# Softmax weights turned in 32 by 32 blocks and carried by DMA, with the gate's products on TensorE, in a cross-attention and expert kernel

## The chip, the cores and the metric

The kernel runs on one core of one Trainium2 chip. The metric is the device time of one execution in microseconds: the median of three runs for the kernel before, and one further execution that a hardware profiler recorded. PE is TensorE, DVE is VectorE, ACT is ScalarE, POOL is GpSimd and SP is SyncE, which here only issues DMAs.

## The reference

One layer of gated cross-attention, followed by a mixture of experts. All data is float32.

```python
# x (32, 112, 256), ctx (32, 375, 256); 16 heads of 64; 8 experts of width 1024, the best 2 of them
lat = layer_norm(layernorm(x)) * g_l + b_l          # 112 latents per batch: the queries
med = layer_norm(ctx) * g_m + b_m                   # 375 rows
q = lat @ Wq
k, v = split(concat([med, lat]) @ Wkv)              # 487 keys per batch
attn = softmax(q @ k.T * 64 ** -0.5)                # per batch and head: 112 x 487
x = x + tanh(g_xattn) * (concat_heads(attn @ v) @ Wout)
xn = layernorm(x)
scores = softmax(xn @ gate_w)                       # 8 experts per token
top2, idx = top_k(scores, 2); top2 /= sum(top2)
y = sum over the two: top2 * (gelu(xn @ w1[e] + b1[e]) @ w2[e] + b2[e])
x = x + tanh(g_ffn) * y
```

## The kernel before

The work has two parts. The first is attention over 32 batches, in a loop over 128 steps n (line 1370). One step handles the softmax of one batch for two pairs of heads, so four heads; `heads_of` (445) says which. Eight steps make a group g of two batches, and m is the step's place in it. The second part, from line 1551 on, is the expert layer over blocks of gathered tokens.

K and V of two batches are computed together by `seven` (361): seven products on PE in place of eight, whose sums DVE and POOL form. Its parts p1, p6, p7, p5 and then three `last` parts are spread over the five slots of a step, K's in one step and V's in the next. The last part p5 ends with two additions on POOL (`add`, 402).

Softmax runs one step ahead. In step n `scores(n + 1)` (451) puts 112 x 487 scores of a pair of heads into PSUM and DVE finds their maxima; `exps` (472) takes the exponentials on ACT into `ex`, with queries on partitions; `norm` (487) multiplies by the reciprocal sums on ACT, for the first pair in slot 1 and for the second in slot 3. Within step n, `turn_attn(n, h)` (494) then turns the weights of the step's own heads: per head four PE transposes of 112 x 122, written to PSUM, and one copy to `exT`, on DVE for three heads and on ACT for one. In every even step `attend` (505) multiplies V with the turned weights of the two steps before, which gives the heads' outputs, in 64 matmul records.

When a tile of 128 tokens is complete, `project` (539), `residual` (556) and `normed` (574) finish attention for it, and `logits_of` (581) forms the gate's eight products per token as eight multiply-and-sum instructions on DVE. `route_parts` (603) finds the two experts, and POOL scatters the rows to DRAM.

The order of instructions is written out by hand (`manual_schedule`, 1262). Each engine runs its instructions in the order in which the program names them, and so does SP's queue of DMAs. In a step that order is: loads for a later batch and zero fills of the gathered rows (`fill`, 168; three at n = 4, three at n = 8, two at n = 12, 3.64 MB each), then for n from 44 to 108 the weight pieces (`piece_out`, `piece_in`, 1204 to 1257: four stores to DRAM and two loads per step; POOL forms their sums in slots 2 and 3), then `attend`, `scores` and `exps` of the next step, and the slots. At n = 126 `others` (1183) takes over the space of the attention weights and loads the first expert's weights and three blocks of rows, all from SP.

Of the kernel before, what the change touches and what calls it, by code (L numbers as in the profile page):

```python
# [18 lines left out]
DH = 64  # L19
# [4 lines left out]
def kernel(  # L24
# [56 lines left out]

    NCK = 4
    KC = (NK + NCK - 1) // NCK
    NKP = NCK * KC
    keys = [(c * KC, min(KC, NK - c * KC)) for c in range(NCK)]

# [16 lines left out]
    gwd = dram.tile([E, D], F32, name="gwd")  # L103
# [60 lines left out]
    gw_sb = const.tile([P, E, D], F32, name="gw_sb")  # L164
# [10 lines left out]
    if True:  # L175
# [9 lines left out]
        ps_s = at.enter_context(tc.tile_pool(name="ps_s", bufs=2, space=PSUM))  # L185
# [105 lines left out]

        def turn(b, k, eng=None):

            if b % 2 == 0 and k == 0:
                kvT[b // 2] = kvp.tile([P, KD, 2, NKP], F32, tag="kvT", name=f"kvT_{b}")
                nc.gpsimd.memset(kvT[b // 2][:, :, :, NK:], 0.0)
            ps = ps_m.tile([P, 512], F32, tag="m", name=f"ps_turn_{b}_{k}")
# [16 lines left out]
        def q_unit(g, i):  # L314

            qT[g, i] = qk.tile([P, 2, S], F32, tag="qT", name=f"qT_{g}_{i}", bufs=6)
# [9 lines left out]
            nc.scalar.mul(qT[g, i], ps, DH**-0.5)  # L326
# [9 lines left out]
        def input_sums(g):  # L336

            (a0, b0), (a1, b1) = ([kvT[g][:, k, u, :] for u in range(2)] for k in range(KD))
            tT[g] = kvp.tile([P, 4, NKP], F32, tag="tT", name=f"tT_{g}")
            t1, t2, t3, t4 = (tT[g][:, n, :] for n in range(4))  # L340
# [20 lines left out]
        def seven(kv, j):  # L361
# [5 lines left out]
            (a0, _), (a1, b1) = ([kvT[g][:, k, u, :] for u in range(2)] for k in range(KD))  # L367
            t1, t2, t3, t4 = (tT[g][:, n, :] for n in range(4))
            v = {}

            def new(at, n):
                if kv == 0:
                    if n is None:
                        v[at] = qk.tile([P, NK], F32, tag="tmpk", name=f"tmpk_{j}", bufs=1)
# [4 lines left out]
                elif n is None:  # L379
                    v[at] = qk.tile([KC, NCK, P], F32, tag="tmpv", name=f"tmpv_{j}", bufs=1)  # L380
                else:
                    v[at] = vv[j][:, :, n[0] - a, n[1] // NG, :]

            def product(n, w, x):
# [5 lines left out]
                else:  # L390
                    ps = ps_m.tile([KC, NCK, P], F32, tag="m", name=f"ps_v_{j}_{n}")
                    for c in range(NCK):
                        nc.tensor.matmul(  # L393
                            ps[:, c, :],
                            lhsT=x[:, c * KC : (c + 1) * KC],
# [9 lines left out]
            def p1():  # L405
                if kv == 1:
                    vv[j] = proj.tile([KC, NCK, 2, 2, P], F32, tag="vv", name=f"vv_{j}")
# [30 lines left out]
        pss, nmx, ex, sm, exT = {}, {}, {}, {}, {}  # L438

        exs = [[const.tile([S, 2, NKP], F32, name=f"ex_{n}_{p}") for p in range(2)] for n in range(2)]  # L440
        for n in range(2):
            for p in range(2):
# [1204 lines left out]
```

## Time and profile before

| | |
|---|---|
| median of three runs | 2115.97 us (2115.82 to 2121.14) |
| profiled execution | 2118.11 us |
| its span, granted clock | 2116.3 us, 0.998 |
| DMA moved | 193.89 MB, mean 92 GB/s |

The span is the time from the first to the last instruction in the trace; the execution's own time includes a little around it. In lines of the profile, "L499" is a line of the kernel, "x2048" the number of instructions, and the names are those of the tiles. The heaviest groups that the change touches, from the page:

| line | engine | what | count | busy us | mean ns |
|---|---|---|---|---|---|
| L499 | PE | transposes of the weights | 2048 | 281.0 | 259 |
| L503 | DVE | copy of the turned weights | 384 | 237.0 | 617 |
| L503 | ACT | the same, one head in four | 128 | 66.3 | 518 |
| L586 | DVE | the gate's products | 224 | 116.4 | 520 |
| L478 | ACT | exponentials, 487 columns | 512 | 337.5 | 667 |
| L492 | ACT | normalisation, 487 columns | 512 | 331.1 | 694 |
| L468 | DVE | maxima, 974 elements | 256 | 287.9 | 1166 |

Busy time of PE is modelled: it takes in the pipeline's latency, so that matmuls overlap in it. The distance between the starts of two instructions is what one of them costs a full queue.

### The profile page before, as it was taken

To read this page: it belongs to the slowest core of one execution; us is meant where nothing else is said; L and a number is where in the kernel's file an instruction comes from. 1 tells how busy PE (TensorE), PEld (TensorE's weight loads), DVE (VectorE), ACT (ScalarE), POOL (GpSimd) and SP (SyncE) were. 2 spreads that over 40 slices of the span, in tenths; PEclk is the share of its full clock that TensorE was granted. 3 is DMA by queue.
4 is the path that set the end of the run, shared out by engine and by line. 5 is a ranking of instruction groups with operands and counts; after the bars stand their busy time and mean duration, and the time that the engine had idled before them with its cause. 6 is when DMAs were issued, how large, how long until landed. Compare 5 with 4: busy or idle time off the path is not lost. (4 is left out here: it accounts for less than half of the span.)

```text
span 2116.3 us, 44362 instructions
## 1 busy us (share of the span) xinstructions
PE 2084.2 (98%) x16232; PEld 1644.0 (78%) x16232; DVE 1367.9 (65%) x2985; ACT 1194.0 (56%) x2817; POOL 965.8 (46%) x1412
## 2 busy tenths in 40 slices
PE   9999999999999999999999999999999999999998
PEld 5777777777777777777777777777777799999887
DVE  6667676767676767676767676767666578655211
ACT  5666565656665666566666666565655433444433
POOL 5532323333345544554535553653233367877312
PEclk9999999999999999999999999999999999999999
DMA  6693000000002211221112211120002257699773
GB/s 151 186 321 109 15 16 18 13 22 27 18 25 65 86 41 53 63 82 53 55 55 58 73 55 55 57 76 4 8 4 68 98 152 221 170 322 299 195 213 59
DMA packets 201027, 193.89 MB, mean 92 GB/s; under 512 B 25856, under 2 KB 170824, under 8 KB 200680
## 3 DMA queue, kind: packets, MB, share of 16 engines
q1 hardware_dynamic: 188344, 174.65, 27.1%
q0 software_dynamic: 11328, 15.33, 3.7%
q8 instruction: 130, 2.13, 0.4%
q10 hardware_dynamic: 1136, 1.05, 0.2%
q14 instruction: 89, 0.73, 0.1%
HBM read 168.20 MB, written 65.76 MB: 111 GB/s over the span
## 5 line engine op out<-in xcount | busy, mean ns | idle before, releaser
L492 ACT ACTIVATE ex<-ex,rc 112x487 f32<-112x487 f32 x512 | 331.1, 694 | 328.2 <-DVE rc L490 325.3
L468 DVE TENSOR_REDUCE nmx<-ps_s 112x2 f32<-112x974 f32 x256 | 287.9, 1166 | 311.9 <-PE ps_s L458 310.9
L478 ACT ACTIVATE ex<-ps_s,nmx 112x487 f32<-112x487 f32 x512 | 337.5, 667 | 159.7 <-DVE nmx L468 157.3
L499 PEld LDWEIGHTS ps_t<-ident,ex 112*122 112x122 f32 x2048 | 232.4, 138 | 120.1 <-issue 96.4
L499 PE MATMUL ps_t<-ident,ex 112*122 112x112 f32 x2048 | 281.0, 259 | 1.0 <-ACT h L1001 1.0
L403 POOL TENSOR_TENSOR vv<-tmpv,vv 122x512 f32<-122x512 f32 x64 | 81.4, 1271 | 415.1 <-ACT vv L421 331.5
L503 DVE COPY exT<-ps_t 122x448 f32<-122x448 f32 x384 | 237.0, 617 | 37.9 <-PE ps_t L499 36.7
L458 PE MATMUL ps_s<-kT,qT 64*112 64x487 f32 x1024 | 242.0, 591 | 0.0
L513 PEld LDWEIGHTS ps_o<-exT,vv 122*64 122x64 f32 (+1 forms) x4096 | 197.6, 136 | 44.8 <-DVE kT L417 33.0
L513 PE MATMUL ps_o<-exT,vv 122*64 122x112 f32 (+1 forms) x4096 | 211.4, 260 | 0.0
L393 PE MATMUL ps_v<-wkv_s,tT 128*122 128x128 f32 x1536 | 202.3, 275 | 1.2 <-DVE vv L417 1.2
L403 POOL TENSOR_TENSOR kT<-tmpk,kT 128x487 f32<-128x487 f32 x63 | 76.8, 1219 | 269.7 <-ACT kT L421 269.7
L387 PE MATMUL ps_k<-tT,wkv_s 128*128 128x487 f32 x378 | 189.4, 583 | 4.1 <-ACT qT L326 3.5
L393 PEld LDWEIGHTS ps_v<-wkv_s,tT 128*122 128x122 f32 x1536 | 181.9, 185 | 4.2 <-issue 1.8
L393 PEld LDWEIGHTS ps_v<-wkv,kvT 128*122 128x122 f32 x1024 | 125.8, 185 | 74.3 <-issue 56.7
L1018 POOL DMA_INDIRECT out_dram<-y,xs x60 | 93.5, 1559 | 156.9 <-DVE y L1042 93.6
L427 DVE TENSOR_TENSOR kT<-ps_k,kT 128x487 f32<-128x487 f32 x189 | 124.6, 659 | 48.2 <-PE ps_k L387 41.9
L427 DVE TENSOR_TENSOR vv<-ps_v,vv 122x512 f32<-122x512 f32 x192 | 131.5, 685 | 35.5 <-PE ps_v L393 28.4
L458 PEld LDWEIGHTS ps_s<-kT,qT 64*112 64x112 f32 x1024 | 81.1, 172 | 79.5 <-issue 63.2
L393 PE MATMUL ps_v<-wkv,kvT 128*122 128x128 f32 x1024 | 139.0, 279 | 1.0 <-DVE kT L427 1.0
L387 PE MATMUL ps_k<-kvT,wkv 128*128 128x487 f32 x252 | 130.2, 598 | 0.0
L1243 POOL TENSOR_TENSOR piece<-piece 128x128 f32<-128x128 f32 x256 | 120.0, 469 | 16.5 <-DMA piece<-in_L_ffn_w_dram 2.5
(288 smaller groups left out, 3943.8 us busy)
## 6 DMA issues: line engine op xcount, KB each, us to landing
w<-in_L_ffn_w_dram SPq DMA_DIRECT2D x132, 256.0 KB
xg<-pad SPq DMA_DIRECT2D x8, 3640.0 KB
w_s<-ws SPq DMA_DIRECT2D x80, 256.0 KB
w_t<-ws SPq DMA_DIRECT2D x80, 256.0 KB
w_b2x<-in_L_ffn_w_dram SPq DMA_DIRECT2D x38, 512.0 KB
piece<-in_L_ffn_w_dram SPq DMA_DIRECT2D x128, 128.0 KB
ws<-piece SPq DMA_DIRECT2D x256, 64.0 KB
cin<-in_ctx_dram SPq DMA_DIRECT2D x32, 336.0 KB
```

Of the source, the lines that this page charges most:

```text
L387: nc.tensor.matmul(ps, lhsT=w[:, 0, i * P : (i + 1) * P], rhs=x[:, :NK], start=True, stop=True)
L393: nc.tensor.matmul(ps[:, c, :], lhsT=x[:, c * KC : (c + 1) * KC], rhs=w[:, 1, i * P : (i + 1) * P], start=True, stop=True,)
L403: nc.gpsimd.tensor_tensor(v[o], v[l], v[r], ALU.add)
L427: nc.vector.tensor_tensor(v[at], product(n, w, x), v[at], ALU.add)
L458: nc.tensor.matmul(ps[:, j, :NK], lhsT=qT[b // 2, i][r, b % 2, :], rhs=kT[b, i][r, :], start=True, stop=True,)
L468: nc.vector.tensor_reduce(nmx[b, i], pss[b, i][:, :, :NK], AX.X, ALU.max, negate=True)
L478: nc.scalar.activation(t[:, j, :NK], ps[:, j, :NK], AF.Exp, bias=nmx[b, i][:, j : j + 1], accum_out=sm[b, i][:, j : j + 1],)
L492: nc.scalar.mul(ex[b, i][:, j, :NK], ex[b, i][:, j, :NK], rc[:, j : j + 1])
L499: nc.tensor.transpose(ps[:, c, :], ex[b, i][:, j, c * KC : (c + 1) * KC], ident[:S, :S])
L503: (nc.scalar.copy if h == 2 else nc.vector.tensor_copy)(exT[b, i, j], ps)
L513: nc.tensor.matmul(ps[y * DH : (y + 1) * DH, r, x * S : (x + 1) * S], lhsT=vv[j][:m, c, x, r, y * DH : (y + 1) * DH], rhs=exT[2 * g + x, i ...
L1243: nc.gpsimd.tensor_tensor(o, l, r, op) for o, l, r, op in ops
```

## The change

PE no longer turns the softmax weights. The queries of a batch are laid out as four blocks of 32 partitions with 28 queries each (the other four hold zeros), and the keys as four chunks of 128, each of four blocks of 32; the PSUM columns behind the 487 keys hold -1e30, so their weights are zero. DVE turns all 32 by 32 blocks of a pair of heads at once and in place (`turn_blocks`, one instruction per pair). What then lies on partitions 32a to 32a + 31 are keys, for query block a; `send_blocks` carries each block row to the partitions of its keys, with 16 DMAs per step, each from 32 partitions to 32 partitions with 2 KB per partition (64 KB). `exT` becomes one tile per step, in three buffers.

In the order of the program `turn_blocks(n + 1, 0)` stands in slot 3 of step n behind the normalisation of the second pair; `turn_blocks(n, 1)` and `send_blocks(n)` are the first things of step n, ahead of its loads, fills and pieces. `attend` reads `exT` of the two steps before it, as it did.

The gate's products become two PE transposes of the normalised rows, a copy on ACT, two matmuls with eight columns and a small copy on DVE per tile of tokens, and the normalisation of these rows moves from DVE to POOL. The gate's matrix is loaded directly, without the turn through DRAM and the broadcast.

The rest follows from the layout: V is kept in chunks of 128 keys and the inputs `kvT` and `tT` get zeros behind the last column; the two score banks in PSUM are fixed tiles that the expert layer shares; and the expert layer keeps some of its temporary tiles in the two `ex` tiles. In step 123 two parts of `seven` change slots.

```diff
     NCK = 4
-    KC = (NK + NCK - 1) // NCK
-    NKP = NCK * KC
-    keys = [(c * KC, min(KC, NK - c * KC)) for c in range(NCK)]
+    NKP = NK + 1
+    NKF = NCK * P
+    keys = [(c * P, min(P, NK - c * P)) for c in range(NCK)]
+    QB, QW, Q = 4, 32, S // 4
...
-        ps_s = at.enter_context(tc.tile_pool(name="ps_s", bufs=2, space=PSUM))
+        ps_s = at.enter_context(tc.tile_pool(name="ps_s", bufs=1, space=PSUM))
+        banks = [ps_s.tile([P, 2, NKF], F32, name=f"bank_{n}") for n in range(2)]
...
-            nc.scalar.mul(qT[g, i], ps, DH**-0.5)
+            nc.scalar.mul(
+                qT[g, i][:, :, :, :Q], ps.rearrange("p u (a i) -> p u a i", a=QB), DH**-0.5
+            )
...
-        exs = [[const.tile([S, 2, NKP], F32, name=f"ex_{n}_{p}") for p in range(2)] for n in range(2)]
+        exs = [const.tile([P, QB, 2, NCK, 2, QW], F32, name=f"ex_{n}") for n in range(2)]
         for n in range(2):
-            for p in range(2):
-                nc.gpsimd.memset(exs[n][p][:, :, NK:], 0.0)
+            nc.vector.memset(banks[n][:, :, NK:], -1.0e30)
+        turns = list(range(6))
+        qTs = const.tile([P, len(turns), 2, QB, QW], F32, name="qTs")
+        nc.gpsimd.memset(qTs, 0.0)
...
                 nc.scalar.activation(
-                    t[:, j, :NK],
-                    ps[:, j, :NK],
+                    exs[n % 2][:, :, p, :, j, :],
+                    ps[:, j, :].rearrange("p (c k r) -> p k c r", c=NCK, r=QW),
                     AF.Exp,
...
             for j in range(2):
-                nc.scalar.mul(ex[b, i][:, j, :NK], ex[b, i][:, j, :NK], rc[:, j : j + 1])
-        def turn_attn(n, h):
-            b, i, j = heads_of(n)[0], heads_of(n)[1][h // 2], h % 2
-            ps = ps_m.tile([KC, NCK, S], F32, tag="m", name=f"ps_t_{b}_{i}_{j}")
-            for c in range(NCK):
-                nc.tensor.transpose(
-                    ps[:, c, :], ex[b, i][:, j, c * KC : (c + 1) * KC], ident[:S, :S]
-                )
-            exT[b, i, j] = soft.tile([KC, NCK, S], F32, tag="exT", name=f"exT_{b}_{i}_{j}", bufs=9)
-            (nc.scalar.copy if h == 2 else nc.vector.tensor_copy)(exT[b, i, j], ps)
+                t = exs[n % 2][:, :, p, :, j, :]
+                nc.scalar.mul(t, t, rc[:, j : j + 1])
+        def turn_blocks(n, p):
+            t = exs[n % 2][:, :, p].rearrange("p k c j r -> p k (c j r)")
+            nc.vector.transpose(t, t)
+        def send_blocks(n):
+            exT[n] = soft.tile([P, QB, 2, NCK, 2, QW], F32, tag="exT", name=f"exT_{n}", bufs=3)
+            for a in range(QB):
+                for k in range(QB):
+                    nc.sync.dma_start(
+                        exT[n][k * QW : (k + 1) * QW, a], exs[n % 2][a * QW : (a + 1) * QW, k]
+                    )
...
                             nc.tensor.matmul(
-                                ps[y * DH : (y + 1) * DH, r, x * S : (x + 1) * S],
+                                ps[y * DH : (y + 1) * DH, r, x * S : (x + 1) * S].rearrange(
+                                    "p (a i) -> p a i", a=QB
+                                ),
                                 lhsT=vv[j][:m, c, x, r, y * DH : (y + 1) * DH],
-                                rhs=exT[2 * g + x, i + r * NG, y][:m, c, :],
+                                rhs=exT[2 * j + x][:m, :, r, c, y, :Q],
...
-        def normed(i):
+        def normed(i, eng=nc.gpsimd):
             g, j = group[i]
-            nc.vector.tensor_scalar(
+            eng.tensor_scalar(
                 xr[g][:, j, 0, :D], x1[i], mvx[i][:, 0, 0:1], rsx[i], ALU.subtract, ALU.mult
             )
...
-        def logits_of(i, lo, hi):
-            g, j = group[i]
-            for e in range(lo, hi):
-                junk = rt.tile([P, D], F32, tag="junk", name=f"junk_{i}_{e}", bufs=1)
-                nc.vector.tensor_tensor_reduce(
...
+        def gate_turn(i):
+            g, j = group[i]
+            ps = ps_m.tile([P, KD, P], F32, tag="m", name=f"ps_gt_{i}")
+            for k in range(KD):
+                nc.tensor.transpose(ps[:, k, :], xr[g][:, j, 0, k * P : (k + 1) * P], ident)
+            xgT[i] = rt.tile([P, KD, P], F32, tag="junk", name=f"xgT_{i}", bufs=1)
+            nc.scalar.copy(xgT[i], ps)
+        def gate_scores(i):
+            ps = ps_m.tile([P, E], F32, tag="m", name=f"ps_g_{i}")
+            for k in range(KD):
+                nc.tensor.matmul(
+                    ps,
+                    lhsT=xgT[i][:, k, :],
+                    rhs=gate_sb[:, k, :],
...
+            nc.vector.tensor_copy(lg[:, i, :], ps)
...
-        nc.sync.dma_start(gwd, gate_w.rearrange("d e -> e d"), allow_slow_non_contiguous=True)
-        nc.sync.dma_start(gw_sb, gwd.unsqueeze(0).to_broadcast([P, E, D]))
+        nc.sync.dma_start(gate_sb, gate_w.rearrange("(k p) e -> p k e", p=P))
...
         for n in range(LAST):
+            turn_blocks(n, 1)
+            send_blocks(n)
             if n % NG == 0:
...
                 if m == m_:
                     dve[0].append(lambda i=i: normed(i))
-                    for h in range(1, 4):
-                        dve[h].append(lambda h=h, i=i: logits_of(i, 2 * h - 2, 2 * h))
+                    pe[3].append(lambda i=i: gate_turn(i))
                 if m == m_ + 1:
-                    dve[0].append(lambda i=i: logits_of(i, 6, 8))
+                    pe[0].append(lambda i=i: gate_scores(i))
...
-                turn_attn(n, h)
                 if more and h in (1, 3):
                     norm(n + 1, h // 2)
+                if more and h == 3:
+                    turn_blocks(n + 1, 0)
```

## Prediction

> **What bounds the kernel now.** I read the page's busy times first, then the busy times by stage, then the order of time in one stretch of the attention part, and last SP's own queue. Part 1 of the page:
>
> ```profile
> PE 2084.2 (98%) x16232; PEld 1644.0 (78%) x16232; DVE 1367.9 (65%) x2985; ACT 1194.0 (56%) x2817; POOL 965.8 (46%) x1412
> ```
>
> TensorE has work all the time. By stage (columns: stretch, length, then PE, PEld, DVE, ACT, POOL busy, granted clock, DMA share, GB/s):
>
> ```profile
> 200.00:565.00 365.00, 363.30 (x2827) 272.92 (x2824) 255.65 (x568) 222.65 (x518) 125.73 (x181) 1.00 0.05 16
> 565.00:1390.00 825.00, 821.55 (x6411) 615.30 (x6410) 578.26 (x1251) 510.89 (x1194) 414.74 (x684) 1.00 0.20 59
> ```
>
> Both are attention: PE is over 99% busy, DVE 70%, the DMA engines 5% and 20%. Matmul ends are modelled, so I take PE's cost from start to start. Two steps n in order of time (start, length):
>
> ```profile
> 701.34 3.30 PE L513 MATMUL ps_o<-exT,vv 122*64 122x112 f32 x64
> ...
> 704.57 1.89 PE L458 MATMUL ps_s<-kT,qT 64*112 64x487 f32 x8
> ...
> 708.18 0.55 PE L499 MATMUL ps_t<-ident,ex 112*122 112x112 f32 x4
> ...
> 708.57 0.94 PE L319 MATMUL ps_q<-kvT,wq_sb 128*128 128x224 f32 x4
> ...
> 714.88 1.89 PE L458 MATMUL ps_s<-kT,qT 64*112 64x487 f32 x8
> ```
>
> An `attend` takes 3.23 us (701.34 to 704.57), a step without it 10.31 (704.57 to 714.88), four transposes 0.39 (708.18 to 708.57). A pair of steps is 10.31 + 10.31 + 3.23, about 23.8; `attend` starts at 75.50, 99.31 and 123.12 agree. Eight steps (one value of g) last 104.5 us (151.34 to 255.28 is 103.9, and 565 to 1390 is 825/8 = 103.1): two plain pairs of 23.8, one of 25.2 with turned inputs, one of 31.7 with two projections of 3.6.
>
> **What goes.** 128 steps x 16 transposes at 0.39/4 us: 1.55 us a step, 12.4 in eight, **198 us of PE**. Also 384 DVE copies of 617 ns (237 us), 128 ACT copies of 518 ns (66 us), and 224 gate products on DVE with their reads (116 + 18 = 134 us).
>
> **What comes on the engines.**
> - DVE: 256 block turns of 128x1024 in place. No row shows one. The 512-element addition takes 685 ns and the 974-element reduction 1166: slope 1.04 ns, offset 0.15, so 1.22 us for 1024. Bounds: 0.69 (two elements at once, the 512-element row) and 2.33 (two passes, twice the 974 row). I take 1.22, nearest to the reduction: 312 us, less than the 371 removed.
> - ACT: 1024 activations grow from 487 to 512 columns, about 5% of their 668 us: +34, against 66 removed. The permuted access could cost more, up to twice 694 ns; or nothing. I take 5%.
> - PE, gate: 28 tiles x (two transposes; L969's four take 0.44 from start to start, so 0.22; two products with 8 columns, between nothing and L650/L651's 0.38): about 0.6 each, 17 us. Scores, K and V products keep their moving columns and so their time.
> - POOL: normalising moved there, 28 x between 0.41 (its 128x256 copy) and 0.94 (twice its 128x128 addition). Off the path while PE reads it three slots later.
>
> With that alone eight steps would need 104.5 - 12.4 + 1.2 = 93.3 us of PE.
>
> **What comes on SP, the real price.** Per step `send_blocks` issues 16 DMAs of 64 KB, all in SP's queue, behind a wait for the second block turn. Prices of SP's queue, in order of time:
>
> ```profile
> 714.41 1.78 SPq L1254 DMA_DIRECT2D ws<-piece  x4
> 717.43 1.76 SPq L1212 DMA_DIRECT2D piece<-in_L_ffn_w_dram  x2
> ```
>
> Four DMAs of 64 KB take 1.78 us to issue: 0.445 each, 7.1 us for 16 (lower bound: the shortest single issue of that line, 0.356, so 5.7; upper: its 3.83 us for four in another stretch, 15.3). L1212 waits until they have landed: the last was issued at 715.75, so landing takes at most 1.7 us. I keep 0.445 and 1.7.
>
> A plain odd step starts its scores at s. Today the second normalisation ends at s + 1.45 (715.04 + 1.29 against 714.88). The two turns then end at about s + 2.9, the first DMA leaves at s + 3.0, the last at s + 3.0 + 15 x 0.445 = s + 9.7, and lands at s + 11.4. The next `attend` needs this tile only in its second quarter, so it may start at s + 10.6; PE reaches it at s + 10.31 - 1.55 = s + 8.75. **PE waits 1.85 us**, about 0.85 where inputs are turned in the odd step (two of four). Per eight steps 5.4: 93.3 + 5.4 = 98.7, a gain of 5.8. An even step has 3.2 us more and hides its DMAs. In `attend` every later PE instruction is queued behind the wait. On DVE the maxima of the next scores stand behind the second turn, 1.8 us later than today (s + 2.9 for 1.12); the exponentials behind them had 1.6 us of idle time ahead of the next normalisation, so I cost that at nothing; without that idle it would be 1.8 us a step. Outside the piece stage there are about 7.9 such groups (n below 44 and above 108): **-45 us**.
>
> **Stage of the pieces (n = 44 to 108, 8 groups).** Here SP already issues, each step, four piece stores (1.78), a wait for them (1.25) and two loads (0.9): 3.95. With 7.1 that is 11.1 a step, 88.6 in eight, plus 4.3 of other loads and stores: 93 against PE's 93.3. SP becomes as busy as PE, and the loads now leave after the block DMAs. POOL's piece sums wait for them (load landed 12.4 us after the sends began), then come 2.1 us of sums and two additions of 1.22, which stand behind them on POOL, then DVE's three additions, normalisation and turns, some 5.5 to 7 us. That circle of two steps is 22.5 to 24 us. I take 24 for plain pairs (today 23.8), 25 and 29.2 for the others: 102.2 against 104.5, **-18 us** in all.
>
> **Fills.** SP also holds the eight zero fills of 3.64 MB, at n = 4, 8, 12:
>
> ```profile
> 76.10 19.55 SPq L172 DMA_DIRECT2D xg<-pad  x3
> 95.69 11.46 SPq L537 DMA_DIRECT2D x<-in_x_dram  x1
> ...
> 109.03 23.03 SPq L172 DMA_DIRECT2D xg<-pad  x3
> ```
>
> Three fills keep the queue 33 us (76.10 to 109.03), by the page's 321 GB/s 34. Today nothing PE needs soon is behind them. After the change the sends of the next, odd step are: they land about 34 + 5.5 us after the fills start, that is 48 us after the sends of the step of the fills, and PE reaches that `attend` after 19. It waits about 28 us at n = 4, 25 at n = 8 (a projection of 3.6 comes between) and 17 at n = 12, where two fills take 11.5 less: **+70 us**.
>
> **End.** At n = 126 `others` puts 12.3 us of expert loads (1664.30 to 1676.6 in SP's queue) ahead of the last sends. From the sends of 126: 7.1 + 12.3 + 7.1 + 1.7, less what runs before: the last `attend` starts some 30 us after the one before it, today 20.3 (1665.29 to 1685.61): **+10**, and +3 for the transposes counted as saved above. The expert stage itself keeps its products; only buffers move. The gate's table no longer goes through DRAM (SP waited 20.3 us for it at the start); nothing on PE waited for that, so nothing.
>
> **Sum.** On the profiled execution's 2118.1 us (span 2116.3, median of three 2116.0): -45 - 18 + 70 + 13 = +20, 2138; against the median **2136**.
>
> **The skill against the rows.** The row for a block turn is the 1.22 us above. The Trainium skill, "VectorE: DVE Perf Modes", The three transpose paths, gives 311 ns for 128x128 on VectorE, bf16, in 32x32 blocks; by eight of those a turn would be an estimated 2.5 us, five a step, DVE would have more work than PE and the kernel would be some 100 us slower than forecast. No run here shows it. The second row is the granted clock of 1.00 in both stages, where PE never pauses. The skill, "TensorE: Matmul & The Clock Gate", Why this matters for your kernels, says that an idle gap above about 3 us halves the clock; by it the three fill stalls and the last one would each cost an estimated 2 to 4 us more, the waits of 1.85 us nothing. The sum above holds none of this.
>
> **Rivals.**
> - *The DMAs land in time, faster.* If issue and landing are nearer 0.36 and 1.2 us, the odd step's chain shortens by 1.8 us and PE hardly waits: 93.3 to 95 per group, SP has room in the pieces, so -9 to -11 in 16 groups, -160, with fills and end unchanged: about 2040; halfway, with the pieces only partly relieved, 2080. For it: the shortest issues on the page, and SBUF as target on both sides, where my landing row writes HBM. Against: back to back the queue shows 0.445.
> - *The block turn takes two passes, slower.* At 2.33 us two turns end at s + 4.7 in place of s + 2.9: 1.8 us more at each of 64 `attend`s, 115, less some 10 that projections and turned inputs hide: about 2240. It counts from 1.45 us on, where the first turn is no longer hidden behind the second normalisation.
> - *The pieces' circle is longer, slower.* If POOL's sums or the stores' landing add 2 us a pair (in the busy stretches L1257's four take 3.83), 32 pairs give +64: 2200.
> - *The change does nothing to PE's time:* the instructions go for certain; only waiting can refill them, which is the forecast itself.
>
> **Chances.** Forecast (2100 to 2170): 0.45, of which 0.08 within 0.3% and 0.04 below that; DMAs in time, fully or half (2030 to 2100): 0.32; longer circle (2170 to 2215): 0.13; two-pass turn: 0.10. What a measurement tells from no change is about 0.3%, 6 us. Faster 0.36, same 0.08, slower 0.56. The range leaves out the best of the first rival and the worst of the second: 2045 to 2230. The likeliest case's own range is 2100 to 2170.
>
> **What would show it.** Steps: PE waiting for DMA of `exT` at `attend`, 1 to 2 us in plain groups; three waits of 17 to 28 us before 300 us; one of about 13 before the experts; SP's issues back to back at 0.445; the turn near 1.22 us; DVE near 1310 us. Wrong it would be if PE stays above 97% outside the fills (the DMAs are hidden), if a fill's waits are short (the queue lets later DMAs pass), or if DVE's turn is far off 1.22.

## The result and the profile after

The changed kernel takes **2486.28 us** in the median of four runs (2485.03 to 2488.9) against 2116.36 us for the kernel before (four runs, 2115.82 to 2121.14): a ratio of 1.174, 95% interval 1.172 to 1.176. That is slower by 370 us, far above the range of 2045 to 2230. The profiled execution took 2488.9 us with a span of 2487.2.

Part 1 of the page of the changed kernel, and the row of the granted clock from part 2:

```profile
PE 2064.7 (83%) x14352; PEld 1583.5 (64%) x14352; DVE 1331.5 (54%) x2413; ACT 1157.8 (47%) x2717; POOL 991.8 (40%) x1467
...
PEclk9887899999998989898989898988899878999999
```

The 2048 transposes are gone and the gate's 168 instructions have come (16232 to 14352 on PE), and every engine is less busy in share than before. No engine took over as the bound: PE now waits 17% of the time, and its clock, 9 in all slices before, dips to 7 and 8.

The starts of successive `attend`s (L539) give the time by stage. "Without sends" is an experiment told below: the changed kernel without its block DMAs.

| stage (n) | before | after | difference | forecast | without sends |
|---|---|---|---|---|---|
| start to `attend` 7 (n = 16; fills) | 223.6 | 317.2 | +93.6 | +59 | 207.1 |
| to `attend` 21 (n = 44; plain) | 371.9 | 400.7 | +28.8 | -20 | 336.7 |
| to `attend` 53 (n = 108; pieces) | 832.6 | 1017.9 | **+185.4** | -18 | 753.3 |
| to `attend` 63 (n = 128) | 257.6 | 300.1 | +42.6 | -1, with the next row | 230.8 |
| to the end (experts) | 430.7 | 451.2 | +20.5 | | 438.9 |

The busy times by stage, plain stage and stage of the pieces (columns as in the prediction: stretch, length, then PE, PEld, DVE, ACT, POOL busy, granted clock, DMA share, GB/s):

```profile
317.00:718.00 401.00, 355.80 (x2463) 261.95 (x2464) 253.69 (x434) 219.95 (x509) 130.83 (x188) 0.94 0.35 90
718.00:1736.00 1018.00, 830.36 (x5510) 586.52 (x5512) 565.99 (x971) 499.45 (x1156) 435.71 (x728) 0.91 0.43 115
```

PE was busy 363 of 365 us before; now it is busy 356 of 401 and 830 of 1018. DVE, ACT and POOL have 33 to 63% of work, the DMA engines 35 to 43%. So nothing that computes or carries is full. What is full is SP's queue, in which all block DMAs stand. Its order of time in the stage of the pieces (start, length of the issues, x how many):

```profile
1009.10 10.83 SPq L527 DMA_DIRECT2D exT<-ex  x16
1020.03 1.98 SPq L1296 DMA_DIRECT2D ws<-piece  x4
1023.29 0.90 SPq L1254 DMA_DIRECT2D piece<-in_L_ffn_w_dram  x2
...
1024.82 10.02 SPq L527 DMA_DIRECT2D exT<-ex  x16
```

From send to send is 15.7 us, twice that 31.4 for a pair of steps. The 16 sends of a step (L527) take 10.0 to 10.8 us, 0.63 to 0.68 each, where the forecast had 0.445 and 7.1. Counted over the whole stage, 64 steps of 15.9 us, SP issues for 13.9 us a step (sends 0.65 each, 10.4; piece stores 2.0; piece loads 0.9; the rest 0.6) and waits 2.0, of which 1.65 are for the piece's stores to land before its loads may go. Ahead of the sends, where it would wait for the block turns, that is for the engines, it waits 0.2 us a step.

Who waits for whom, over the whole execution (total us, times, longest):

```profile
POOL piece L1285 <- DMA piece<-in_L_ffn_w_dram: 543.3, 71, 11.4
...
PE ps_o L539 <- DMA exT<-ex: 201.0, 36, 32.4
```

The largest wait is POOL's for the piece loads, which stand behind the sends. PE's own for the blocks is 201 us, of which 82 are three waits at the fills.

The row of the operation that no row showed before, the block turn, in the costliest groups (busy us, mean ns, idle before):

```profile
L520 DVE STREAM_TRANSPOSE ex<-ex 128x1024 f32<-128x1024 f32 x256 | 315.0, 1230 | 29.8 <-ACT ex L515 29.2 <-issue 0.6
```

1.230 us each; the forecast had 1.22 from the neighbouring rows.

### The profile page after: what moved, and what is told of

The parts are those of the page before. It is cut to its first block, busy times and chain, and to the rows that moved or that the text cites. A ratio compares the mean times of both kernels' runs of the same rounds, so it can differ in the third digit from the quotient of the medians.

```text
span 2487.2 us, 43679 instructions
## 1 busy us (share of the span) xinstructions
PE 2064.7 (83%) x14352; PEld 1583.5 (64%) x14352; DVE 1331.5 (54%) x2413; ACT 1157.8 (47%) x2717; POOL 991.8 (40%) x1467
## 5 line engine op out<-in xcount | busy, mean ns | idle before, releaser
L515 ACT ACTIVATE ex<-ex,rc 128x512 f32<-128x512 f32 x512 | 342.1, 717 | 370.1 <-DVE rc L512 360.2
L492 DVE TENSOR_REDUCE nmx<-bank 128x2 f32<-128x974 f32 x256 | 286.2, 1158 | 408.2 <-PE bank L482 408.2
L539 PE MATMUL ps_o<-exT,vv 128*64 128x112 f32 (+1 forms) x4096 | 302.5, 318 | 219.9 <-DMA exT<-ex 201.0
L539 PEld LDWEIGHTS ps_o<-exT,vv 128*64 128x64 f32 (+1 forms) x4096 | 276.0, 176 | 292.0 <-issue 184.9
L501 ACT ACTIVATE ex<-bank,nmx 128x512 f32<-128x512 f32 x512 | 348.7, 689 | 240.1 <-DVE nmx L492 223.7
L520 DVE STREAM_TRANSPOSE ex<-ex 128x1024 f32<-128x1024 f32 x256 | 315.0, 1230 | 29.8 <-ACT ex L515 29.2
L482 PE MATMUL bank<-kT,qTs 64*128 64x487 f32 x1024 | 250.0, 607 | 0.0
L412 PEld LDWEIGHTS ps_v<-wkv_s,tT 128*128 128x128 f32 x1536 | 192.1, 192 | 56.5 <-issue 49.1
L412 PE MATMUL ps_v<-wkv_s,tT 128*128 128x128 f32 x1536 | 196.3, 276 | 4.4 <-DVE kT L446 4.1
L412 PE MATMUL ps_v<-wkv,kvT 128*128 128x128 f32 x1024 | 141.4, 281 | 0.0
```

Source lines behind the costliest of these rows:

```text
L412: nc.tensor.matmul(ps[:, c, :], lhsT=x[:, c * P : (c + 1) * P], rhs=w[:, 1, i * P : (i + 1) * P], start=True, stop=True,)
L482: nc.tensor.matmul(ps[:, j, :NK], lhsT=qT[b // 2, i][r, b % 2].rearrange("p a i -> p (a i)"), rhs=kT[b, i][r, :], start=True, stop=True,)
L492: nc.vector.tensor_reduce(nmx[b, i], pss[b, i][:, :, :NK], AX.X, ALU.max, negate=True)
L501: nc.scalar.activation(exs[n % 2][:, :, p, :, j, :], ps[:, j, :].rearrange("p (c k r) -> p k c r", c=NCK, r=QW), AF.Exp, bias=nmx[b, i][:, ...
L515: nc.scalar.mul(t, t, rc[:, j : j + 1])
L520: nc.vector.transpose(t, t)
```

## The experiments

**Theory A:** the time is lost in SP's one in-order queue, by the number of its issues and what each costs, not by bytes. **Rival B:** the bytes, in flight or landing. **Rival C:** POOL's pieces and normalised rows, or DVE's turns, bind. **Rival D:** the fallen clock of PE is a cause and not a consequence. All kernels but `gate_only` and `best` were executed once, on a chip on which the kernel before took 2117 to 2118 us. A "pair" of steps below is the mean over the 32 pairs of the piece stage: 26.0 before, 31.8 after. (The 24 of the prediction was for plain pairs alone; with the wide ones its mean was 102.2/4 = 25.6.)

### The gate alone, and everything but the sends

`gate_only` puts the gate's part of the diff alone into the kernel before; `no_sends` is the changed kernel with

```
-            exT[n] = soft.tile(...)
-            for a in range(QB):
-                for k in range(QB):
-                    nc.sync.dma_start(exT[n][k * QW : ..., a], exs[n % 2][a * QW : ..., k])
+            exT[n] = still[n % 3]        # three constant tiles of zeros
```

> The kernel before with the gate part alone: two transposes, a copy on ACT and two products with 8 columns per row tile in place of the DVE products, and the normalisation on POOL. The softmax weights are still transposed on TensorE. Theory A (the block DMAs' time in SP's queue is the loss, the gate is small): 28 x 0.6 us of PE, less a little DVE relief, so 2116 + 5 to 17, about 2128. Rival C (the gate's transposes wait for POOL and hold up everything queued behind them on PE; in the changed kernel nine such waits of up to 9.3 us sum to 46, with the weight loads 51): the same waits appear here, and the time is 2116 + 17 + 30 to 50, about 2165 to 2185.

> The changed kernel without the 2048 block DMAs: attend reads three constant tiles of zeros, so the attention's output is left out; block turns, products and gate stay. Theories A and B (the loss is the block DMAs, by their issue or by their bytes): the piece stage falls from 31.8 us a pair to 22 to 24, the three waits before 320 us vanish, and the whole takes 2116 - 198 (transposes) + 17 (gate) + 0 to 50 = 1935 to 1985 us. Rival C (POOL's pieces and the normalised rows, or DVE's turns, bound it): the piece stage stays above 26 us a pair and the time above 2100.

Measured: `gate_only` 2131.05 us, a ratio of 1.0063 (1.0046 to 1.0080), so +13 us; `no_sends` 1968.6 us with a pair at 23.5. The gate costs in sum what was forecast (where it costs it is told below). All else that the change does, block turns, wider activations and products included, is worth 148 us of gain; the 2048 block DMAs and what waits for them cost 518 us. The rows of `no_sends` by stage, plain and pieces:

```profile
207.00:544.00 337.00, 334.12 (x2467) 244.16 (x2468) 253.73 (x435) 219.81 (x509) 131.10 (x188) 1.00 0.07 20
544.00:1297.00 753.00, 745.84 (x5508) 542.74 (x5504) 571.55 (x967) 496.01 (x1154) 440.01 (x732) 1.00 0.23 67
```

PE is busy 99% in both at a clock of 1.00, with the same pieces and the same block turns as in the changed kernel. Rival C, POOL or DVE as the bound by themselves, is out.

### Fewer bytes, or fewer DMAs

`half_bytes` sends only the first head pair of each block (16 DMAs of 32 KB a step), `half_count` sends two blocks with each DMA (8 of 128 KB):

```
half_bytes:  exT[n][k * QW : ..., a, 0]      <- exs[n % 2][a * QW : ..., k, 0]
half_count:  exT[n][k * QW : ..., a : a + 2] <- exs[n % 2][a * QW : ..., k // 2 * 2 : k // 2 * 2 + 2],  a in (0, 2)
```

> The changed kernel with 16 block DMAs a step as before, each of 32 KB in place of 64 (the second head pair's weights are left out and read as zeros). Theory A (SP's issue per DMA): the 16 still take about 10 us of SP's queue, the piece stage stays at 30 to 32 us a pair, the time at 2440 to 2490. Rival B (bytes in flight): the issue falls to about 5 us for 16, the piece stage to 24 to 26 us a pair, the time to 2180 to 2280.

> The changed kernel with 8 block DMAs a step of 128 KB in place of 16 of 64: the same bytes to the same partitions, but blocks of the wrong key quarter for half of them, so the attention's output is not the reference's. Theory A (SP's issue per DMA, 0.6 us whatever its size): 8 take about 5 us, the piece stage falls to 23 to 25 us a pair (from 31.8), that is 220 to 280 us less there, and with the fills' waits remaining (about 80) the time is 2180 to 2260. Rival B (bytes): each DMA takes 1.2 us, 8 take 10 us, the time stays at 2440 to 2490.

Measured: `half_bytes` 2419.7 us, a pair at 31.5; `half_count` **2123.9 us**, a pair at 25.2 and no wait between `attend` 7 and 21. SP's queue in `half_bytes` (first fence) and `half_count` (second):

```profile
913.63 11.09 SPq L530 DMA_DIRECT2D still<-ex  x16
...
929.07 11.00 SPq L530 DMA_DIRECT2D still<-ex  x16
```

```profile
915.64 4.95 SPq L527 DMA_DIRECT2D exT<-ex  x8
...
927.71 4.96 SPq L527 DMA_DIRECT2D exT<-ex  x8
```

Half the bytes in as many DMAs take as long to issue (11.0 for 16); the same bytes in half as many take half (4.95 for 8, 0.62 each, at twice the size). The time follows: 67 us less by the first, 362 less by the second. That is the whole of the loss against the kernel before within 8 us, and more than was expected; 155 us remain to the kernel without sends. Of the 67 us, 36 stand in the plain stage, so the bytes cost something there. Theory A holds, rival B as the main cause is out.

### What one issue costs

`micro` computes nothing of the layer; it issues groups of 2 to 8 DMAs of one form, each from an idle queue (only L90 follows L87 at once).

> None of the computation: x is copied to the output, and SP's (once ACT's) queue issues groups of 8 DMAs of one form each, every group after all earlier ones have landed, three times over. It measures why a block DMA took 0.62 us to issue where a 64 KB piece store took 0.445, and what else is to be had. Reading A1 (the price belongs to moving to other partitions): 32 partitions x 2 KB between tiles in SBUF take 0.62 each when the partitions change and 0.45 when they stay. Reading A2 (it belongs to SBUF as source and target): 0.62 for all such DMAs, 0.45 for those from or to DRAM whatever their shape. Reading A3 (it belongs to the shape of 32 partitions): 0.62 with DRAM on one side too, 0.45 for 128 partitions x 512 B in SBUF. Reading A4 (the wait for the DMA eight before): 0.45 or less everywhere here, as no group is longer than eight.

Measured, lines of the second of three rounds that agree to 0.3 us a group (the forms: L78 32 partitions x 2 KB to other partitions in SBUF, L81 the same to the same partitions, L84 128 partitions x 512 B in SBUF, L87 the same to DRAM, L90 32 x 2 KB to DRAM, L93 32 x 2 KB from DRAM, L102 1 MB to DRAM, L111 32 x 512 B in SBUF):

```profile
147.31 4.94 SPq L78 DMA_DIRECT2D dst<-src  x8
157.13 4.94 SPq L81 DMA_DIRECT2D dst<-src  x8
166.96 5.02 SPq L84 DMA_DIRECT2D dst<-src  x8
174.18 3.67 SPq L87 DMA_DIRECT2D big<-src  x8
177.95 3.67 SPq L90 DMA_DIRECT2D big<-src  x8
185.74 3.55 SPq L93 DMA_DIRECT2D dst<-big  x8
...
210.94 0.80 SPq L102 DMA_DIRECT2D big<-src  x2
...
239.75 4.99 SPq L111 DMA_DIRECT2D dst<-src  x8
```

With SBUF on both sides a DMA takes 0.62 us to issue, whatever its shape, its size (16 to 64 KB here, 128 KB in `half_count`; four of 256 KB took 2.42 us) and whether the partitions change. With DRAM on one side it takes 0.44 to 0.46, 0.40 for 1 MB. That is reading A2. ACT's queue took 5.05 to 5.07 us for 8 of the form of L78: the same price. The row that I had priced the sends by, L1254's four stores, writes DRAM.

### The sends at the price that was forecast

`sends_cheap` sends 15 of the 16 blocks to a scratch tile in DRAM:

```
+                    to = aside[n % 4][a, k]
+                    if a == k == QB - 1:
+                        to = exT[n][k * QW : (k + 1) * QW, a]
+                    nc.sync.dma_start(to, exs[n % 2][a * QW : (a + 1) * QW, k])
```

> The changed kernel with 15 of the 16 block DMAs of each step going to a scratch tile in DRAM (64 KB each, as before) and only the last to the tile that attend reads, whose other blocks are zeros: 15 of 16 blocks are left out of the attention's output. In the small measurement a DMA of this form takes 0.46 us to issue, so 7.5 us for 16, near the 7.1 that the forecast had; attend still waits for the landing of the last. If only the issue price was wrong in the forecast: a pair takes 23.5 to 25 us in the piece stage (31.8), the fills' waits stay at 65 to 80 and the time is 2110 to 2170. If the circle through POOL was modelled too short as well: 26 us a pair or more, 2190 or more.

Measured: 2284.8 us, a pair at 27.8. The step's SP queue:

```profile
1017.73 1.97 SPq L1301 DMA_DIRECT2D ws<-piece  x4
1021.08 0.90 SPq L1259 DMA_DIRECT2D piece<-in_L_ffn_w_dram  x2
1023.11 6.89 SPq L534 DMA_DIRECT2D aside<-ex  x15
1030.10 0.51 SPq L534 DMA_DIRECT2D still<-ex  x1
```

0.16 us less per issue gives 201 us in all and 4.0 of the 6.2 us by which a pair exceeded the forecast's 25.6. The 201 are too few: this kernel leaves most of the attention's output out, so its tokens are routed otherwise: PE has 150 more matmul records behind the last `attend` (14502 in place of 14352) and that stage takes 475 us in place of 451. Up to the last `attend` the gain is 228 us. The rest is a miss of my expectation: it falls on the side "26 us or more". The queue's own count says why, and it is not POOL: SP issues 11.3 us a step here and waits 2.6 (1.64 for the stores' landing, 0.67 for turns), 13.9 in all. The forecast had 11.6: the sends are still at 0.488 (+0.7), the waits for turns were not in it (+0.7), the wait for the landing is longer than its 1.25 (+0.4), and the piece stores take 2.0 and not 1.78 (+0.2).

### The pieces: merged, and moved ahead

`pieces_merged` makes one store of each piece's four and, for the second layer, one load of two. `pieces_first` changes the order of a step in the queue only:

```
             turn_blocks(n, 1)
+            piece_out(k - 1)
+            piece_in(k)
             send_blocks(n)
...
-                piece_out(k - 1); piece_in(k)        (from behind the sends)
```

> The changed kernel with each piece's four stores of 64 KB made one of 256 KB (the scratch matrices' four slots in another order), and its two loads one for the second layer's half of the pieces. The bytes, the sums on POOL and the wait between store and load stay. Theory A (issues in SP's queue): 3 to 4 issues fewer a step, 1.4 to 1.8 us of the queue, 2.8 to 3.6 a pair, so 31.8 falls to 28 to 29 and the time by 90 to 115 to about 2385. Rival C (POOL's sums and additions close the circle, or the landing does): less than 30 us gained.

> The changed kernel with the order of one step's DMAs in SP's queue turned round: the piece's stores and the next piece's loads ahead of the step's 16 block DMAs in place of behind them. Nothing is added or left out. If the piece stage is bound by the circle through POOL (the loads leave after the sends, POOL's sums wait for them, its additions stand behind the sums, then DVE's additions, the turn and the next sends), POOL's wait for pieces (543 us) falls by more than half and a pair takes 26 to 28 us (31.8): the time is 2300 to 2370. If it is bound by the sum of SP's issues and the wait between store and load (about 14 to 14.5 us a step), a pair stays at 28 to 29.5: 2370 to 2420. If only the late sends count, PE waits for the blocks in place of DVE, a pair takes 31 or more and the time is above 2460.

Measured: `pieces_merged` 2421.6 us, a pair at 30.0, 65 us less where 90 to 115 were expected; SP issues 12.3 us a step in place of 13.9, but the wait between store and load grows from 1.65 to 2.2, since fewer issues stand ahead of it; a third of what the fewer issues save is given back there. `pieces_first` 2489.8 us, a pair at 31.9: **nothing**. Its waits:

```profile
PE ps_o L539 <- DMA exT<-ex: 307.3, 52, 32.3
...
POOL piece L1285 <- DMA piece<-in_L_ffn_w_dram: 158.9, 36, 10.4
```

POOL's wait for pieces fell from 543 to 159 us as the circle theory asks, and PE's wait for blocks rose from 201 to 307 in its place. SP's count is 13.7 us of issues and 2.3 of waits a step, as before to 0.3. So the longest wait of the table was no cause: whichever of the two kinds of DMA goes first, the other is late. By its time this is the third case of the expectation; it is the count that says that the sum of the queue sets the step. My figure for that sum (14 to 14.5, with the wait) was too small: the issues alone take nearly 14.

### The clock

`warm` adds four products of constants ahead of the last slot in each odd step of the piece stage.

> The changed kernel with four products of constants (128x128 by 512 columns, about 1 us each, read by nobody) ahead of the last slot's products in each odd step n = 45 to 107: PE works through most of the wait of 4 to 5 us that stands there. Rival D (the granted clock falls to 0.5 after such a wait and the slower products lengthen the circle: PE's busy time in the changed kernel is 141 us above that of the kernel without sends, for the same products): a pair falls from 31.8 to 29 to 31 us and the time by 25 to 90 us, though PE has 128 more products. If the slow products lie beside the wait for SP's queue and cost nothing, the time stays within 15 us; where PE was not waiting the four add up to 4 us a pair, 2500 to 2610.

Measured: 2494.3 us, +8. The rows of the piece stage, of `warm`:

```profile
717.00:1745.00 1028.00, 905.56 (x5766) 608.99 (x5764) 568.77 (x970) 503.03 (x1157) 435.46 (x728) 0.95 0.42 114
```

The granted clock rose from 0.91 to 0.95, and PE did 256 more matmul records (the 128 added products) in a stage that became 10 us longer. Neither helped: in this stage the slow products lie beside SP's queue, which hardly waits for an engine. Rival D is out there. It is not out in the plain stage, which `warm` did not touch. Two steps of the changed kernel in it:

```profile
571.24 1.90 PE L482 MATMUL bank<-kT,qTs 64*128 64x487 f32 x8
...
580.85 0.99 PE L539 MATMUL ps_o<-exT,vv 128*64 128x112 f32 x16
584.05 4.18 PE L539 MATMUL ps_o<-exT,vv 128*64 128x112 f32 x48 [2.21 <-DMA exT<-ex]
588.16 1.90 PE L482 MATMUL bank<-kT,qTs 64*128 64x487 f32 x8
```

After a wait of 2.21 us the 48 products take 4.18 us, where they take 2.53 after short waits, and the next scores stand behind them. The row of these 4.18 us has a granted clock of 0.59 (columns as above); within them it is 0.50 from 584.58 to 587.99 and 1.00 before and after:

```profile
584.05:588.23 4.18, 4.18 (x50) 4.00 (x50) 0.00 (x0) 0.00 (x0) 3.94 (x5) 0.59 0.33 83
```

Here the sends had begun at 571.53 and taken 10.79 us, and `attend` went on at 584.05, 1.7 us after the last issue. Per eight steps of the plain stage (114.5 us): 96.2 as without sends, 12.1 of waits, and 6.2 by which PE's products are longer than without sends.

### The fills

`fills_apart` cuts the eight fills into 32 and gives them to ACT's queue:

```
-                for _ in range(fills.get(b, 0)):
-                    fill(filled)
+            if 4 <= n < 4 + 4 * E:
+                dve[1].append(lambda: fill_part(n - 4))   # nc.scalar.dma_start, 0.91 MB
```

> The changed kernel with the eight zero fills of 3.64 MB cut into 32 of 0.91 MB, one in each step n = 4 to 35, issued from ACT's queue in place of SP's; the same bytes go to the same place. Theory A (the order of one queue): the waits of 32.5, 28.7 and 20.9 us at the attends of n = 6, 10 and 14 fall to 2 to 5 each, ACT pays 1.5 to 2.5 us in each of 32 steps beside PE's work, and the time falls by 60 to 85 to about 2410. Rival B (the fills' bytes hold up the block DMAs wherever they are issued): waits of the same sum, spread over n = 4 to 35, and the time stays above 2460.

Measured: 2438.9 us, 47 us less. In the changed kernel SP's fills and PE's wait behind them (two views, SP's queue and PE's order of time):

```profile
94.50 19.54 SPq L174 DMA_DIRECT2D xg<-pad  x3
114.15 51.59 SPq L527 DMA_DIRECT2D exT<-ex  x48
```

```profile
105.13 0.99 PE L539 MATMUL ps_o<-exT,vv 128*64 128x112 f32 x16
138.57 4.75 PE L539 MATMUL ps_o<-exT,vv 128*64 128x112 f32 x48 [32.45 <-DMA exT<-ex]
```

The three waits were 32.5, 28.7 and 20.9 us, 82 in all (forecast 28, 25 and 17, 70). With the fills apart the `attend`s before n = 16 wait 3 to 6 us and that stage is 64 us shorter; but the next one, in which fills now run until n = 35, is 22 us longer. So the order of the queue made the three long waits. Why the next stage grew, by the fills' bytes (rival B, in part) or by something else, was not tried.

### Two queues

`two_queues` gives every second block to ACT's queue: `(nc.sync, nc.scalar)[k % 2].dma_start(...)`.

> The changed kernel with every second block DMA issued from ACT's queue. If 0.62 us is the issuing engine's own time: 8 take about 5 us on SP and as much on ACT, side by side; SP is relieved, ACT has 7.8 + 5 us of work a step in the piece stage and its exponentials come later, so a pair takes 25 to 28 us and the time is 2200 to 2330. If the rate of such DMAs is shared by all queues (one per 0.62 us in all): 16 still take 10 us from first to last, a pair stays at 30 us or more, the time above 2430.

Measured: 2361.9 us, a pair at 28.5, between the two cases of the expectation. SP's eight take 5.3 to 6.8 us while ACT issues its own at 0.61 each, so the price is the issuing engine's own. But ACT's sends stand in its instructions' order and wait there for the turn, with the exponentials and copies behind them: PE waits 98 us for ACT's copies of K (none before), and SP is no longer full (9.0 us of issues and 5.2 of waits a step). The Trainium skill, "DMA: Bandwidth & Descriptors", Issuing engines are not separate DMA queues, says that a second engine saves only the time to initiate a DMA, "usually small relative to the DMA itself". Here that time is 10.4 us a step against 1.7 us of landing, and it is what binds.

### Through DRAM

`bounce` stores each turned head pair whole (512 KB) in DRAM and loads it by key quarter, so that the rearrangement is done on DRAM's side, where one DMA can cover four blocks: 10 DMAs a step for 16, twice the bytes. `bounce_order` has the same DMAs in another order.

```
+        def hop_in(n, p):
+            nc.sync.dma_start(hops[n % 4][p], exs[n % 2][:, :, p]...)
+        def hop_out(n, p):
+            for k in range(QB):
+                nc.sync.dma_start(
+                    exT[n][k * QW : (k + 1) * QW, :, p]...,
+                    hops[n % 4][p, :, k].rearrange("(a i) f -> i a f", a=QB),
+                )
bounce:        hop_out(n, 0); hop_in(n, 1); piece_out; hop_out(n, 1); piece_in; hop_in(n + 1, 0)
bounce_order:  hop_in(n, 1); piece_out; hop_out(n, 0); hop_out(n, 1); piece_in; hop_in(n + 1, 0)
```

> The changed kernel with the blocks carried through DRAM: for each head pair one store of 512 KB as soon as its turn is done (the first pair's already in the step before), then four loads of 128 KB, one for each 32 key partitions. So 10 DMAs a step for 16 and twice the bytes. Theory A (issues in one queue): about 4.5 to 5 us of SP's queue a step for 10, the piece stage at 23 to 25 us a pair, the fills' waits (70 to 85 in all) as they were; the time is 2100 to 2160. Rival B (bytes): 2 MB a step beside the pieces' 0.5 MB need more than the engines give, loads land late, the piece stage stays at 28 us a pair or more and the time above 2300.

> The kernel that carries the blocks through DRAM, with SP's queue in another order: the second pair's store first, then the piece's stores, then the eight loads of blocks, then the piece's loads, so that neither wait for a landing (3.3 us each) holds up a store behind it. Same DMAs, same bytes. Theory A (order and waits of the one queue): a step's queue falls from 12.9 us to 8 to 10, a pair from 27.4 to 23 to 24.5 and the time from 2306 to 2170 to 2210. Rival B (bytes in flight): a pair stays at 26 to 27.5.

Measured: `bounce` 2306.1 us, a pair at 27.4, a miss; `bounce_order` **2152.5 us**, less than expected, though a pair at 25.4 is above the 23 to 24.5 expected. In `bounce`:

```profile
1007.71 0.52 SPq L525 DMA_DIRECT2D hop<-ex  x1
1011.49 1.81 SPq L532 DMA_DIRECT2D exT<-hop  x4
1013.39 0.52 SPq L525 DMA_DIRECT2D hop<-ex  x1
1014.01 2.48 SPq L1305 DMA_DIRECT2D ws<-piece  x4
1018.01 1.75 SPq L532 DMA_DIRECT2D exT<-hop  x4
```

A step's issues are down to 8.9 us, but the queue stands still for 4.8: from 1008.23 to 1011.49 for the landing of a store that has only just left. The second pair's store stands behind that; its turn ended at 1007.98, and it left at 1013.39. In the other order issues come between store and load, the waits fall to 3.8 us a step, some 2.9 for turns and 0.9 for POOL's sums, and 154 us are gained without a DMA less. The kernel moves 461 MB in place of 327 and the DMA engines are busy 78% of the piece stage for 43%; that it is 334 us faster than the changed kernel speaks once more against the bytes. The piece stage of `bounce_order`:

```profile
630.20:1443.50 813.30, 766.17 (x5510) 549.90 (x5509) 569.83 (x969) 497.25 (x1154) 437.28 (x728) 0.99 0.78 226
```

`best` joins what the runs pointed to: `bounce_order`, the fills on ACT's queue, one store per piece, the normalised rows on DVE, and at the end the expert loads behind the last blocks.

> The reordered kernel that carries the blocks through DRAM, with the zero fills in 32 parts on ACT's queue, one store for each piece, the normalised rows on DVE, and the expert loads of the end behind the last blocks (the second layer's matrix of the first unit two steps later). Theory A: a pair at 23 to 24 us in the piece stage, no wait above 6 us before 260 us, 5 to 15 us less at the end: 2030 to 2080 us, a ratio of 0.96 to 0.985 to the kernel before; the floor is 1969, the kernel without sends. Rival B (bytes): waits of 2 to 4 us at most attends remain, 2100 or more.

Measured: **2067.03 us** (four runs, 2059.35 to 2069.5), a ratio to the kernel before of 0.9752 (0.9732 to 0.9772); a pair is at 24.7. It beats both kernels, by 2.5% and 17%. Its piece stage:

```profile
584.00:1373.00 789.00, 758.55 (x5509) 547.28 (x5508) 577.05 (x981) 496.64 (x1154) 419.03 (x714) 0.99 0.82 233
```

PE is busy 96% there (82% in the changed kernel), at a clock of 0.99. 98 us remain to the kernel without sends; how they divide was not tried.

## Why the prediction was wrong

SP's queue was named as the place where the change is paid, but the step **"Four DMAs of 64 KB take 1.78 us to issue: 0.445 each, 7.1 us for 16"** failed. The row was of stores to DRAM; sends inside SBUF took 0.65 in the kernel and 0.62 alone. I had named "SBUF as target on both sides" as a reason why they could be cheaper. They are dearer. The upper bound kept for it (15.3 us for 16, from L1257 and not from the line of the price) held the measured 10.4, but no case of the chances was worked out with it, so the range was cut too short. With the sends near the forecast's price, `sends_cheap` takes 353.7 us in the plain stage, 18 less than the kernel before where 20 less was forecast: there the reckoning was right but for the price. In the stage of the pieces it takes 58 us more than the kernel before where 18 less was forecast: there a second step failed, told below.

- *What goes.* The transposes go, but 198 us was too much: eight steps of the plain stage without sends take 96.2 us, not 93.3, and PE's busy time falls by 161 us from before to the kernel without sends, with 14 of gate in it: about 175.
- *The block turn.* Right: 1.230 against 1.22. The figure worked out from the Trainium skill, "VectorE: DVE Perf Modes", The three transpose paths, 2.5 us, was twice what the trace shows, so its rival of two passes is out. (The prediction says that DVE would then have more work than PE; by its own terms it would have some 1640 us against PE's 1900.)
- *The gate.* Right in sum, +13 against 17, and in part by luck: the 17 were spread over the tiles, but in `gate_only` 4 us stand ahead of the last `attend` and 9 behind it, where PE waits 4.5 us for the last rows and 2.5 for ACT's copy of their turn. The rows' move to POOL, costed at nothing, is not quite that: PE waits 46 us for them in the changed kernel, 9 times, all in the stage of the pieces, where POOL itself is late by SP's queue; in `gate_only` and without sends it never waits for POOL there.
- *"PE waits 1.85 us"* a plain odd step, 5.4 in eight. Measured 12.1 in eight, with 3.7 us more issue before each such `attend`; landing was the 1.7 us forecast. And what the sum held at nothing, the clock after such waits, adds 6.2. So eight plain steps rose from 106.3 to 114.5 where 98.7 was forecast.
- *Stage of the pieces.* "As busy as PE, 93 us in eight steps" was the queue's sum; it is 127. Of the 34 more, the sends' price is 26 and the longer wait between store and load 3; the rest is mostly dearer piece stores and waits for turns. I then took the circle through POOL, 102.2, as the larger and so the bound; `pieces_first` shows that with the true price the plain sum of the queue is larger still, and sets the step alone. Even near the forecast's price it is larger: 13.9 us a step in `sends_cheap`, 111 in eight, against the circle's 102.2. The rival "longer circle" was near in time, 2200, but named the wrong thing.
- *Fills.* Right in kind and place, 82 us for 70.
- *End.* 63 us behind n = 108 in place of -1: 2.4 groups of plain steps with the fault above (some 20 more, not 14 less), waits of 10.2, 6.2 and 7.0 us at the last three `attend`s, with loads for the experts ahead of the sends, where one long wait was forecast, and the gate's 9. `best`, which moves these loads, ends its stages 53 to the end 57 us earlier; how much of that is the loads alone was not tried.
- *The clock.* The Trainium skill, "TensorE: Matmul & The Clock Gate", Why this matters for your kernels, gives a gap of about 3 us as the limit. In the changed kernel, `half_count` and `sends_cheap`, a wait of up to 1.7 us ahead of `attend`'s 48 products, with not more than half a microsecond of other waits in the 10 us before it, left them at 2.53 us; after 1.76 to 2.93 us they took 2.53 in some cases and 3.7 to 4.2 in others (both after 1.76 us in `sends_cheap`); after 3.0 us and more always 3.6 us or more. So here the slow clock always came from the page's limit on, and could come from 1.8 us on. In the prediction the rule stood beside the sum, for the three fills' stalls and the last one; the many waits of 2 to 5 us at plain `attend`s, which the sum did not hold, cost more.

The sum: forecast +20, measured +371 between the two profiled executions; 203 of the difference stand in the stage of the pieces, 49 in the plain stage, 35 before it and 64 at the end.

## What to carry to other kernels

A queue is an engine: before moving work into DMAs, add up each issue and each wait in the queue they go to, step by step, with a price from a row of the same kind (what is source and what is target), and compare the sum with the step; halve the bytes and then the count to see which of them binds. The longest wait in a table need not be on the path: change the order so that it goes, and see whether the time does. Here fewer and larger DMAs with the rearrangement on DRAM's side beat many small ones inside SBUF (2152.5 us against 2486.28, with more bytes), once no wait for a landing stood ahead of ready work in the queue (2306.1 with it).

## What the runs showed of the hardware

- A DMA from SBUF to SBUF takes 0.62 us of SP's or ACT's queue, one with DRAM on a side 0.44 to 0.46 (one store of 1 MB 0.40), in `micro`, independent of its shape and, inside SBUF, of sizes from 16 to 256 KB. In the kernels the sends took 0.65, and 0.49 with DRAM as target.
- The granted clock was 0.50 for 3.4 us after a single wait of 2.21 us, and such falls came after waits from 1.8 us on (see above). In the stage of the pieces, where the queue and not PE sets the step, raising it from 0.91 to 0.95 gained nothing (`warm`); in the plain stage PE's products are 1.6 us a pair longer than without sends.
- VectorE turns 128x1024 fp32 in blocks of 32 by 32, in place, in 1.23 us, near the 1.16 of its reduction of 974 elements.
